# Selective scan on one Trainium2 core: softplus summed in PSUM, one odd group in five multiplied by VectorE, projection begun a third of a step sooner, step sizes in single buffers

## The chip, the cores and the metric

The kernel runs on one core of a Trainium2 chip. A core has TensorE (PE in the profile), VectorE (DVE), ScalarE (ACT), GpSimd (POOL) and SyncE (SP), which here issues all DMAs. The metric is the device time of one execution in microseconds, lower is better; the median of several runs stands for a kernel.

## What is computed

The input x has shape 16 x 64 x 64 x 96, in float32. Two residual layers follow each other. Layer 0 is a group norm, upsampling by Fourier interpolation, two dense layers around a quadratic, a low-pass filter and downsampling. Layer 1, around which the change lies, is a group norm, an input projection, a depthwise 3 x 3 convolution with SiLU, and a selective scan over the 4096 positions in four directions:

```
delta = softplus(dts + dt_bias)                    # per channel and position
h = exp(dt[..., None] * As[None]) * h + (dt * ut)[..., None] * bt[:, :, None, :]
y = einsum('bkdn,bkn->bkd', h, ct)                 # 16 states per channel
```

Four directions x 192 channels x 16 states are 12,288 recurrences of 4096 steps for each of 16 images. A layer norm, a gate and an output projection end the layer.

## The kernel before, in words

The order of instructions on every engine is written out by hand; each engine works its own queue in that order, and semaphores link the queues. There are three generators of background work and one main loop.

**The main loop (scan).** `steps` lists 8 steps per image: four chunks of T = 1024 positions forwards (pair 0), then four backwards (pair 1), 128 steps in all. A step has six blocks (lines 601 to 603), a block has NQ = 4 units j, and so there are 3072 units n, 24 in a step and 192 in an image. A unit holds two groups e = 1 (odd) and e = 0, each 128 recurrences (32 channels x 4 states) over 1024 positions. For a group:

- ScalarE makes the decay exp(delta * a) from SBUF into a PSUM tile `da` (`decay`, L725). There are two such tiles.
- GpSimd multiplies dt * u with B for both groups of a unit at once, from SBUF into SBUF (`drive`, L731: tile `b`, three buffers).
- VectorE runs the recurrence (`recur`, L740 forwards, L742 backwards). For e = 1 the state overwrites `b` in SBUF, for e = 0 it overwrites `da` in PSUM.
- The state is multiplied by C: e = 1 on GpSimd in place (L877)[...], e = 0 on VectorE from PSUM into `b` (L887).
- ScalarE copies the state's last column for the next chunk (`keep`, L748), except in the last chunk of a direction. L877 waits for that copy, since it overwrites what the copy reads.
- TensorE adds up the four states of each channel by 8 matmuls with a 0/1 matrix per group (`read_out`, L764), and `store` (L775) moves the sums out after four units.

The order within one iteration n (lines 869 to 894): scan e = 1 of n, keep, decay (n+1, 1), read_out (n-1), background slot 0, L877 of n, drive (n+2); then scan e = 0 of n, background slot 1, L887 of n, keep, decay (n+1, 0), background slot 2. A buffer of `b` is free for drive (n+2) once read_out (n-1) is done.

**Background work.** In each of the three slots of a unit the class `Background` runs one slice of a generator (up to a `yield`), spread evenly: `step_gen`, and then `ahead_gen` or, once that is finished, `behind_gen`. Slices say how many yields are spread over how many places. `front(mi+1)` is layer 0 and the convolution of the next image; `finish(mi-1)` is layer norm, gate and output projection of the image before; both share SLICES = 540 in 576 places. `project` makes the operands of the next step: it is begun at block 0 and spread as PSLICES = 60 over 59 places, drained at block 5, j = 0.

**project (lines 622 to 677)** works in 2 halves of 512 positions. Three tiles u are fetched, three matmuls (L640) give B, C and the ranks of dt in PSUM, ScalarE copies them to SBUF (L643), and then, for each of three channel tiles, one matmul (L650) gives s, the argument of softplus, in PSUM. Softplus is max(s, 0) + ln(1 + e) - ((1 + e) - 1 - e) with e = exp(-|s|); the last term corrects the rounding of 1 + e. ScalarE computes |s| and e (L658, L659), ln (L661) and 1 + e (L666), VectorE L664, L668 and L669, then dtu = s * u (L672). ScalarE copies delta to SBUF (L674). Both go to HBM (L676, L677). Such a piece occurs 768 times.

**Fetches.** `fetch` (L684) brings dtu and delta of a block, each spread over the four states of a channel, into tiles for both groups: dtu at j = 0 and delta at j = 1 of the block before, from pools of two. `fetch_bc` (L693) brings B and C rows. In `front`, the intermediate of the filter is fetched into two tiles of 44 and 20 columns (lines 408 to 416) and read by L433.

Of the kernel before, what the change touches and what calls it, by code (L numbers as in the profile page):

```python
# [51 lines left out]
C = 96  # L52
HW = 64
# [18 lines left out]
SLICES = 540  # L72
WAIT = -1
HEAVY = 2
PSLICES = 60
# [3 lines left out]
def tile_two_blocks(  # L79
# [103 lines left out]
    b12 = ctx.enter_context(tc.tile_pool(name="b12", bufs=1))  # L183
# [56 lines left out]
    def front(mi):  # L240
# [72 lines left out]
        for p0 in range(0, UPS, PP):  # L313
# [94 lines left out]
        JS = 44  # L408
        s = [
            b18.tile([UPS, JS, C], F32, name="s0", tag="b18"), b12.tile([UPS, HW - JS, C], F32, name="s1", tag="b12")  # L410
        ]
        for _ in range(2):
            yield
        for i, n, first in [(0, JS // 4, k * JS // 4) for k in range(4)] + [(1, 10, 0), (1, 10, 10)]:
            nc.sync.dma_start(out=s[i][:, first:first + n, :], in_=s_d[:, JS * i + first:JS * i + first + n, :])
            yield
# [4 lines left out]
        for j0 in range(0, HW + 8, 8):  # L421
            if done is not None:
                nc.scalar.activation(
                    x1v[:, :, j0 - 8:j0], done.rearrange("c w h -> c h w"), AF.Identity, bias=shift
                )
            if j0 < HW:
                done = bank([C, 8, HW], "e_ps")
                nc.tensor.matmul(
                    done.rearrange("c w h -> c h w"), lhsT=lin, rhs=x1v[:, :, j0:j0 + 8], start=True, stop=False,
                    skip_group_check=True,  # L430
                )
                for j in range(8):
                    nc.tensor.matmul(  # L433
                        done[:, j, :], lhsT=s[(j0 + j) // JS][:, (j0 + j) % JS, :], rhs=down_s, start=False, stop=True,
                        skip_group_check=True,
                    )
            yield
        yield from parts(made["x1"], x1)
# [167 lines left out]
    def scan():  # L606


        with ExitStack() as es:
            pj = es.enter_context(tc.tile_pool(name="sc_pj", bufs=1))  # L610
            up_ = es.enter_context(tc.tile_pool(name="sc_u", bufs=3))
            cp = es.enter_context(tc.tile_pool(name="sc_bc", bufs=5))
            p3 = es.enter_context(tc.tile_pool(name="sc_3", bufs=3))
            p2 = es.enter_context(tc.tile_pool(name="sc_2", bufs=2))
            yp = es.enter_context(tc.tile_pool(name="sc_y", bufs=1))
            stp = es.enter_context(tc.tile_pool(name="sc_st", bufs=2))
            banks.append(es.enter_context(tc.tile_pool(name="b_ps", bufs=2, space=PSUM)))
# [4 lines left out]
            def project(mi, pair, lc, out):  # L622

                out["rows"] = rows = dram.tile([2, 2 * NS, T], F32, name="rows")
                out["delta"] = [dram.tile([128, T], F32, name=f"delta_d{v}") for v in range(3)]
                out["dtu"] = [dram.tile([128, T], F32, name=f"dtu_d{v}") for v in range(3)]
                xs_d = image[mi]["xs"]
                for t in range(0, T, TB):  # L630
                    u = []
                    for v in range(3):
                        uv = up_.tile([128, TB], F32, name="u")
                        nc.sync.dma_start(out=uv, in_=xs_d[v, :, lc * T + t:lc * T + t + TB])
                        u.append(uv)
                    for _ in range(3):
                        yield
                    pp = gps.tile([128, TB], F32, name="pp", tag="g")
                    for v in range(3):
                        nc.tensor.matmul(pp, lhsT=xpt_s[:, pair, v, :], rhs=u[v], start=(v == 0), stop=(v == 2))  # L640
                    yield
                    pr = pj.tile([128, TB], F32, name="pr")
                    nc.scalar.activation(pr, pp, AF.Identity, bias=bumps_s)  # L643


                    for i, v in enumerate((0, 2, 1)):
                        if i == 0:
                            yield
                        s = gps.tile([128, TB], F32, name="s", tag="g")
                        nc.tensor.matmul(s, lhsT=dtw_s[:, pair, v, :], rhs=pr, start=True, stop=True)  # L650
                        if i == 0:
                            for r in range(2):
                                nc.sync.dma_start(
                                    out=rows[r, :, t:t + TB], in_=pr[64 * r:64 * r + 2 * NS, :]
                                )
                        yield
                        e, d = (pj.tile([128, TB], F32, name=k) for k in ("e", "d"))
                        nc.scalar.activation(e, s, AF.Abs)  # L658
                        nc.scalar.activation(e, e, AF.Exp, scale=-1.0)  # L659
                        yield  # L660
                        nc.scalar.activation(d, e, AF.Ln, bias=one_s)  # L661
                        for _ in range(2):
                            yield
                        nc.vector.scalar_tensor_tensor(d, s, 0.0, d, ALU.max, ALU.add)  # L664
                        yield
                        nc.scalar.activation(s, e, AF.Identity, bias=one_s)  # L666
                        yield
                        nc.vector.scalar_tensor_tensor(s, s, -1.0, e, ALU.add, ALU.subtract)  # L668
                        nc.vector.tensor_sub(s, d, s)  # L669
                        dtu = pj.tile([128, TB], F32, name="dtu")  # L670
                        delta = pj.tile([128, TB], F32, name="delta")
                        nc.vector.tensor_mul(dtu, s, u[v])  # L672
                        yield
                        nc.scalar.copy(delta, s)  # L674
                        yield
                        nc.sync.dma_start(out=out["dtu"][v][:, t:t + TB], in_=dtu)  # L676
                        nc.sync.dma_start(out=out["delta"][v][:, t:t + TB], in_=delta)  # L677

            def fetch(what, ctx, bi):

                v, s0, r = blocks[bi]
                t = p2.tile([128, 2, T], F32, name=what)
                for e in (1, 0):
                    nc.sync.dma_start(  # L684
                        out=t[:, e, :],
                        in_=ctx[what][v][32 * (s0 + e):32 * (s0 + e) + 32, :].unsqueeze(1).to_broadcast([32, NQ, T]),
                    )
                return t
# [23 lines left out]
            ops = {(w, 0): fetch(w, ctxs[0], 0) for w in ("dtu", "delta")}  # L712
# [9 lines left out]
            def decay(n, e):  # L722
                k, g = group(n, e)
                da = aps.tile([128, T], F32, name="da")
                nc.scalar.activation(da, ops["delta", n // NQ][:, e, :], AF.Exp, scale=a_s[:, k, g, units[n][2]:units[n][2] + 1])  # L725
                das[n, e] = da

            def drive(n):
                b = p3.tile([128, 2, T], F32, name="b")
                bt = bc[0, blocks[units[n][1]][2], units[n][2]]  # L730
                nc.gpsimd.tensor_mul(b, ops["dtu", n // NQ], bt.unsqueeze(1).to_broadcast([128, 2, T]))  # L731
                bs[n] = b
# [11 lines left out]
            def keep(n, e, h):  # L744
                st, bi, j = units[n]
                if st % NT < NT - 1:
                    end = h[:, T - 1:T] if steps[st][1] == 0 else h[:, 0:1]
                    nc.scalar.copy(states[bi][1][:, e, j:j + 1], end)  # L748
# [77 lines left out]
            last = len(units) - 1  # L826
            for n in range(2):
# [5 lines left out]
            for n, (st, bi, j) in enumerate(units):  # L833
# [11 lines left out]
                if j == 0:  # L845
                    if bi == 0 and st + 1 < len(steps):
                        if steps[st + 1][0] > mi:
                            ahead_gen.drain()
                        step_gen = Background(project(*steps[st + 1], ctxs[st + 1]), PSLICES, 59)
# [3 lines left out]
                if j == 0:  # L853
# [3 lines left out]
                    elif n + NQ <= last:  # L857
                        step_gen.drain()
                        ahead = ctxs[st + 1], 0
                    if ahead:  # L860
                        ops["dtu", m + 1] = fetch("dtu", *ahead)
                elif j == 1:
                    if ahead:
                        ops["delta", m + 1] = fetch("delta", *ahead)
                    if n + NQ <= last and steps[units[n + NQ - 1][0]][1] == 1:
                        st2, bi2, _ = units[n + NQ - 1]
                        y0s[steps[st2][2], bi2] = fetch_y0(steps[st2][2], bi2)

                h = bs[n][:, 1, :]
                recur(n, 1, h)  # L870
                keep(n, 1, h)
                if n < last:
                    decay(n + 1, 1)
                if n:
                    read_out(n - 1)
                slot(0)
                nc.gpsimd.tensor_mul(h, h, bc[1, r, j])  # L877
# [5 lines left out]
                if n and units[n - 1][2] == NQ - 1:  # L883
                    storing = store(n - 1)
# [3 lines left out]
                keep(n, 0, h)  # L888
# [3 lines left out]
                if storing is not None:  # L892
                    next(storing, 0)
                    storing = None

# [9 lines left out]
            read_out(last)  # L905
# [112 lines left out]
```

## Time and profile before

| | us |
|---|---|
| median of 3 runs (21913.64 to 21924.9) | 21916.79 |
| the profiled execution's own time | 21910.69 |
| its span, first to last instruction | 21908.9 |
| PE busy | 15342.2 (70%) |
| ACT busy | 13130.2 (60%) |
| L740, L742: 6144 scans, each | 2.28 to 2.34 |
| L725 decay, each (6144) | 1.116 |
| DMA, mean rate over the span | 195 GB/s |

A row of the page's groups gives line, engine, operation, tiles (output <- inputs), shapes and count; after the bar the busy time in us and the mean of one in ns; after the second bar the time that the engine sat idle just before such instructions, with what ended it. A row of the order of time gives start and length in us, engine, line, operation; in brackets the idle time before it and what ended it. A row of the waits gives who waited for whom: us in total, times, longest. Engines also have weight loads (PEld) and DMA issues (SPq) of their own.

### The profile page before, as it was taken

How to read it: one execution, taken by the hardware profiler on the slowest of the kernel's cores; microseconds unless marked ns; L12 is line 12 of the kernel's file. 1: busy time of each engine (PE TensorE's matmuls, PEld its weight loads, DVE VectorE, ACT ScalarE, POOL GpSimd, SP SyncE). 2: the span in 40 equal slices, each digit the busy share in tenths (PEclk: the TensorE clock that was granted, in tenths of full speed). 3: DMA queues.
4: the chain of work that ended last, by engine and by line, in shares of the span. 5: the costliest groups of instructions: out<-in, count | busy, mean ns of one | idle time of the engine just before them, and what ended most of it. 6: DMA issues, size and time to landing. Idle time of an engine off the chain costs nothing.

```text
span 21908.9 us, 260666 instructions
## 1 busy us (share of the span) xinstructions
PE 15342.2 (70%) x92844; PEld 6324.7 (29%) x92844; DVE 19849.9 (91%) x12829; ACT 13130.2 (60%) x20854; POOL 20900.4 (95%) x6152
## 2 busy tenths in 40 slices
PE   6766767766777677777767677767777677677745
PEld 4322323232232322324233232322323223242211
DVE  0999999999999999999999999999999999999996
ACT  4665656666565665656656566665656656566543
POOL 0999999999999999999999999999999999999997
PEclk7776777877778777777877778777787877778856
DMA  2555565656656566565655656556565655656654
GB/s 80 190 191 188 193 214 194 209 195 200 205 191 215 189 206 201 192 215 192 207 198 194 214 192 209 196 201 206 193 211 189 210 199 198 206 195 208 210 177 134
DMA packets 1851895, 4276.30 MB, mean 195 GB/s; under 512 B 449118, under 2 KB 548350, under 8 KB 1848542
## 3 DMA queue, kind: packets, MB, share of 16 engines
q1 hardware_dynamic: 1850590, 4259.62, 58.1%
q8 instruction: 731, 11.98, 0.2%
q14 instruction: 574, 4.70, 0.1%
HBM read 3380.58 MB, written 878.18 MB: 194 GB/s over the span
## 4 chain that ended last, share of the span: by engine, by line
DVE 36%; POOL 19%; issue 18%; PE 9%; ACT 9%; DMA 7%; SPq 1%; POOLq 0%; DVEq 0%; ACTq 0%
POOL b L731 10%; POOL b L877 10%; DVE da L742 7%; DVE da L740 7%; DVE b L740 6%; DVE b L742 6%; DVE b L887 4%; ACT da L725 4%; DMA u<-xs_d 2%; DVE s L669 2%; DVE dtu L672 2%; DVE s L668 2%; PE y L764 1%; DMA ct<-rows 1%; PE pp L640 1%
## 5 line engine op out<-in xcount | busy, mean ns | idle before, releaser
L731 POOL TENSOR_TENSOR b<-dtu,bt 128x2048 f32<-128x2048 f32 x3072 | 13984.9, 4552 | 584.6 <-DMA dtu<-dtu_d 522.9
L725 ACT ACTIVATE da<-delta,a_s 128x1024 f32<-128x1024 f32 x6144 | 6853.5, 1116 | 2826.6 <-DVE b L887 1185.9
L877 POOL TENSOR_TENSOR b<-b,ct 128x1024 f32<-128x1024 f32 x3072 | 7309.1, 2379 | 259.8 <-ACT new L748 249.5
L764 PE MATMUL y<-b,fold_s 128*32 128x256 f32 x49152 | 4638.9, 492 | 4107.3 <-DVE b L887 3102.6
L887 DVE TENSOR_TENSOR b<-da,ct 128x1024 f32<-128x1024 f32 x3072 | 3752.6, 1222 | 84.5
L764 PEld LDWEIGHTS y<-b,fold_s 128*32 128x32 f32 x49152 | 1353.3, 126 | 7627.7 <-DVE b L887 4083.3
L740 DVE TENSOR_TENSOR_SCAN da<-da,new,b 128x1024 f32<-128x1024 f32 x1152 | 2694.3, 2339 | 252.3 <-ACT da L725 252.3
L740 DVE TENSOR_TENSOR_SCAN b<-da,new,b 128x1024 f32<-128x1024 f32 x1152 | 2698.0, 2342 | 174.1 <-POOL b L731 166.9
L742 DVE TENSOR_TENSOR_SCAN da<-da,new,b 128x1024 f32<-128x1024 f32 x1152 | 2693.8, 2338 | 172.9 <-ACT da L725 172.7
L742 DVE TENSOR_TENSOR_SCAN b<-da,new,b 128x1024 f32<-128x1024 f32 x1152 | 2697.1, 2341 | 151.6 <-POOL b L731 109.5
L748 ACT COPY new<-da 128x1 f32<-128x1 f32 x2304 | 362.3, 157 | 3028.5 <-DVE b L887 3023.2
L473 PE MATMUL c_ps<-xgp,wtap_s 96*128 96x512 f32 (+1 forms) x4608 | 1817.8, 675 | 168.9 <-ACT row L491 164.1
L650 PE MATMUL s<-pr,dtw_s 128*128 128x512 f32 x1536 | 1120.4, 819 | 557.8 <-ACT delta L674 516.7
L377 PE MATMUL o_ps<-w2c_s,hsq 128*100 128x96 f32 x9600 | 1205.3, 293 | 191.9 <-ACT hsq L348 180.1
L365 PE MATMUL h_ps<-xu,w1t_s 96*128 96x500 f32 x1920 | 1147.6, 700 | 244.2 <-ACT hsq L348 108.6
L748 ACT COPY new<-b 128x1 f32<-128x1 f32 x2304 | 432.6, 188 | 1445.7 <-DVE b L742 740.4
L377 PEld LDWEIGHTS o_ps<-w2c_s,hsq 128*100 128x100 f32 x9600 | 1119.5, 203 | 407.4 <-ACT hsq L348 227.7
L640 PE MATMUL pp<-u,xpt_s 128*128 128x512 f32 x1536 | 903.7, 734 | 224.2 <-DMA u<-xs_d 216.0
L742 DVE TENSOR_TENSOR_SCAN b<-da,b 128x1024 f32<-128x1024 f32 x384 | 876.7, 2283 | 133.2 <-ACT da L725 74.8
L473 PEld LDWEIGHTS c_ps<-xgp,wtap_s 96*128 96x128 f32 (+1 forms) x4608 | 631.9, 182 | 1193.3 <-issue 938.6
L740 DVE TENSOR_TENSOR_SCAN da<-da,b 128x1024 f32<-128x1024 f32 x384 | 875.8, 2281 | 106.9 <-ACT da L725 106.9
L742 DVE TENSOR_TENSOR_SCAN da<-da,b 128x1024 f32<-128x1024 f32 x384 | 876.0, 2281 | 105.0 <-ACT da L725 105.0
(120 smaller groups left out, 18077.1 us busy)
## 6 DMA issues: line engine op xcount, KB each, us to landing
dtu<-dtu_d SPq DMA_DIRECT2D x1536, 512.0 KB
delta<-delta_d SPq DMA_DIRECT2D x1536, 512.0 KB
bt<-rows SPq DMA_DIRECT2D x1024, 512.0 KB
ct<-rows SPq DMA_DIRECT2D x1024, 512.0 KB
u<-xs_d SPq DMA_DIRECT2D x896, 256.0 KB
dtu_d<-dtu SPq DMA_DIRECT2D x768, 256.0 KB
delta_d<-delta SPq DMA_DIRECT2D x768, 256.0 KB
xr<-in_x SPq DMA_DIRECT2D x768, 128.0 KB
```

Source lines behind the costliest of these rows:

```text
L365: nc.tensor.matmul(h_ps[j], lhsT=w1t_s[:, 128 * j:128 * (j + 1)], rhs=xu.rearrange("c p q -> c (p q)"), start=True, stop=True,)
L377: nc.tensor.matmul(o_ps[:, p, :], lhsT=hsq[j][:, UPS * p:UPS * (p + 1)], rhs=w2c_s[:, j, :], start=(j == 0), stop=(j == HB - 1),)
L473: nc.tensor.matmul(c_ps[p:p + n], lhsT=wtap_s[:, tap, 128 * i:128 * i + n], rhs=xgp[:, h0:h0 + 8, dx:dx + HW], start=(tap == 0), stop=(tap ...
L640: nc.tensor.matmul(pp, lhsT=xpt_s[:, pair, v, :], rhs=u[v], start=(v == 0), stop=(v == 2))
L650: nc.tensor.matmul(s, lhsT=dtw_s[:, pair, v, :], rhs=pr, start=True, stop=True)
L725: nc.scalar.activation(da, ops["delta", n // NQ][:, e, :], AF.Exp, scale=a_s[:, k, g, units[n][2]:units[n][2] + 1])
L731: nc.gpsimd.tensor_mul(b, ops["dtu", n // NQ], bt.unsqueeze(1).to_broadcast([128, 2, T]))
L740: nc.vector.tensor_tensor_scan(out, da, b, before, ALU.mult, ALU.add)
L742: nc.vector.tensor_tensor_scan(out[:, ::-1], da[:, ::-1], b[:, ::-1], before, ALU.mult, ALU.add)
L764: nc.tensor.matmul(y[32 * q:32 * q + 32, e, :], lhsT=fold_s, rhs=b[:, e, QT * q:QT * q + QT], start=(pair == 0 and j == 0 and e == 0), sto ...
L877: nc.gpsimd.tensor_mul(h, h, bc[1, r, j])
L887: nc.vector.tensor_mul(bs[n][:, 0, :], h, bc[1, r, j])
```

## The change

In words, part by part:

- **SHARE = 5.** In units with n % 5 = 4 the scan of e = 1 writes its state into `da` (PSUM), and VectorE multiplies it by C into `b`. L877 is left out there.
- **Softplus.** ScalarE makes m = max(s, 0), w = 1 - (1 + e) in two instructions, e and d = ln(1 + e); four matmuls with the identity add w + e + d + m in PSUM (the same PSUM buffer as s, after it is read). The three VectorE instructions L664, L668 and L669 and ScalarE's L666 go.
- **keep.** For e = 1 VectorE copies the last column, where the state is in SBUF; ScalarE copies it in the units with n % 5 = 4.
- **project.** Begun at block 5, j = 0 for the step after the next, as 71 slices in 72 places, drained there a step later; u tiles are asked for ahead (four buffers), and their channel order is that of their use. Its HBM tiles come from a pool of three.
- **Buffers.** delta's two groups become single tiles from a pool of three, fetched at j = 1 (e = 1) and j = 3 (e = 0). `b` has four buffers, and read_out and store come a unit later (n-2). y0 is fetched at the end of the unit before its block.
- **front.** The filter's intermediate is fetched in two parts, 40 and 24 columns, into one buffer one after the other; with more yields. SLICES becomes 550.

The diff, cut:

```diff
-SLICES = 540
+SLICES = 550
-PSLICES = 60
+PSLICES = 71
+SHARE = 5
...
+        def fetch_s(first, n):
+            t = b18.tile([UPS, n, C], F32, name="s", tag="b18")
+            for k in range(0, n, 8):
+                nc.sync.dma_start(out=t[:, k:k + 8, :], in_=s_d[:, first + k:first + k + 8, :])
+                yield t, first
+        JS = 40
...
+            if j0 == JS:
+                for s, s_first in fetch_s(JS, HW - JS):
+                    yield
...
+                ahead_u = [fetch_u(v, 0) for v in order]
+                for _ in range(4):
+                    yield
                 for t in range(0, T, TB):
-                    for _ in range(3):
-                        yield
+                    u, ahead_u = dict(zip(order, ahead_u)), []
...
-                        e, d = (pj.tile([128, TB], F32, name=k) for k in ("e", "d"))
+                        e, d, m, w = (pj.tile([128, TB], F32, name=k) for k in ("e", "d", "m", "w"))
                         nc.scalar.activation(e, s, AF.Abs)
                         nc.scalar.activation(e, e, AF.Exp, scale=-1.0)
                         yield
+                        nc.scalar.activation(m, s, AF.Relu)
+                        nc.scalar.activation(w, e, AF.Identity, bias=one_s)
+                        yield
                         nc.scalar.activation(d, e, AF.Ln, bias=one_s)
-                        for _ in range(2):
+                        nc.scalar.activation(w, w, AF.Identity, scale=-1.0, bias=one_s)
+                        yield
+                        s = gps.tile([128, TB], F32, name="s", tag="g")
+                        yield
+                        for k, of in enumerate((w, e, d, m)):
+                            nc.tensor.matmul(s, lhsT=ident_s, rhs=of, start=(k == 0), stop=(k == 3))
+                        for _ in range(3):
                             yield
-                        nc.vector.scalar_tensor_tensor(d, s, 0.0, d, ALU.max, ALU.add)
-                        yield
-                        nc.scalar.activation(s, e, AF.Identity, bias=one_s)
-                        yield
-                        nc.vector.scalar_tensor_tensor(s, s, -1.0, e, ALU.add, ALU.subtract)
-                        nc.vector.tensor_sub(s, d, s)
                         nc.vector.tensor_mul(dtu, s, u[v])
...
-                b = p3.tile([128, 2, T], F32, name="b")
+                b = p4.tile([128, 2, T], F32, name="b")
...
-                    if bi == 0 and st + 1 < len(steps):
-                        if steps[st + 1][0] > mi:
-                            ahead_gen.drain()
-                        step_gen = Background(project(*steps[st + 1], ctxs[st + 1]), PSLICES, 59)
...
                         step_gen.drain()
                         ahead = ctxs[st + 1], 0
+                        next_step(st + 2, mi)
...
                 elif j == 1:
                     if ahead:
-                        ops["delta", m + 1] = fetch("delta", *ahead)
+                        deltas[m + 1, 1] = fetch_delta(*ahead, 1)
+                elif j == 3:
+                    if ahead:
+                        deltas[m + 1, 0] = fetch_delta(*ahead, 0)
...
-                h = bs[n][:, 1, :]
+                odd_here = n % SHARE == SHARE - 1
+                h = das[n, 1] if odd_here else bs[n][:, 1, :]
                 recur(n, 1, h)
-                keep(n, 1, h)
+                if odd_here:
+                    nc.vector.tensor_mul(bs[n][:, 1, :], h, bc[1, r, j])
+                keep(n, 1, h, nc.scalar.copy if odd_here else nc.vector.tensor_copy)
                 if n < last:
                     decay(n + 1, 1)
-                if n:
-                    read_out(n - 1)
+                if n >= 2:
+                    read_out(n - 2)
                 slot(0)
-                nc.gpsimd.tensor_mul(h, h, bc[1, r, j])
+                if not odd_here:
+                    nc.gpsimd.tensor_mul(h, h, bc[1, r, j])
```

`next_step(st, mi)` sets step_gen to `Background(project(...), PSLICES, 3 * per_step)`, 72 places, after draining ahead_gen if the step is one of the next image.

## The prediction

> **What bounds the kernel now.** I read four views in this order: the page's busy times, the groups of instructions, the order of time in the middle of the run, and the list of waits. All durations are of the profiled execution, 21,910.7 us (span 21,908.9), 6 us under the median of the runs, 21,916.8.
>
> The page puts GpSimd (POOL) first and VectorE (DVE) close behind:
>
> ```profile
> PE 15342.2 (70%) x92844; PEld 6324.7 (29%) x92844; DVE 19849.9 (91%) x12829; ACT 13130.2 (60%) x20854; POOL 20900.4 (95%) x6152
> DVE  0999999999999999999999999999999999999996
> POOL 0999999999999999999999999999999999999997
> ```
>
> The missing 5% of POOL is the serial start and end. Busy time by stretch separates them:
>
> ```profile
> 0.00:560.00 560.00, 384.38 (x2340) 229.72 (x2340) 60.93 (x84) 237.48 (x395) 45.58 (x21) 0.78 0.26 81
> 560.00:21760.00 21200.00, 14818.93 (x90216) 6054.10 (x90216) 19772.50 (x12722) 12868.05 (x20420) 20854.84 (x6132) 0.76 0.59 199
> ```
>
> The columns after the length are PE, PEld, DVE, ACT, POOL, clock. In the 21,200 us of the scan POOL idles 345 us and DVE 1,427 us. So POOL sets the pace, with DVE 5% behind it. A unit (n in the main loop; 3072 of them) has one multiplication L877 and one L731 on POOL, and on DVE two scans (b for e=1, then da for e=0) and L887:
>
> ```profile
> L731 POOL TENSOR_TENSOR b<-dtu,bt 128x2048 f32<-128x2048 f32 x3072 | 13984.9, 4552 | 584.6 <-DMA dtu<-dtu_d 522.9
> L877 POOL TENSOR_TENSOR b<-b,ct 128x1024 f32<-128x1024 f32 x3072 | 7309.1, 2379 | 259.8 <-ACT new L748 249.5
> L887 DVE TENSOR_TENSOR b<-da,ct 128x1024 f32<-128x1024 f32 x3072 | 3752.6, 1222 | 84.5
> ```
>
> ```profile
> 10009.03 0.69 DVE L668 SCALAR_TENSOR_TENSOR s<-s,e 128x512 f32<-128x512 f32 x1
> 10009.12 2.35 POOL L877 TENSOR_TENSOR b<-b,ct 128x1024 f32<-128x1024 f32 x1
> ...
> 10009.76 0.70 DVE L669 TENSOR_TENSOR s<-d,s 128x512 f32<-128x512 f32 x1
> 10010.49 0.69 DVE L672 TENSOR_TENSOR dtu<-s,u 128x512 f32<-128x512 f32 x1
> 10011.10 2.34 DVE L740 TENSOR_TENSOR_SCAN b<-da,new,b 128x1024 f32<-128x1024 f32 x1
> ...
> 10011.44 4.50 POOL L731 TENSOR_TENSOR b<-dtu,bt 128x2048 f32<-128x2048 f32 x1
> ```
>
> POOL goes from L877 to L731 in 2.32 us and the next L877 starts at 10015.91: 6.79 us a unit, with no gap. The waits show what DVE loses when it isn't waiting for POOL:
>
> ```profile
> DVE da L740 <- ACT da L725: 359.2, 285, 5.9
> DVE da L742 <- ACT da L725: 277.6, 267, 2.4
> POOL b L877 <- ACT new L748: 249.5, 168, 4.0
> DVE b L740 <- POOL b L731: 216.8, 270, 1.1
> DVE b L742 <- POOL b L731: 166.5, 198, 1.1
> ```
>
> **What the Trainium skill says.** (1) "SBUF — State Buffer", Who interferes with whom: GpSimd's SBUF ports are VectorE's second pair; a VectorE instruction with two SBUF inputs, or one in a two-port mode, and a GpSimd instruction lock each other out for a whole instruction. The trace agrees: L259, with two SBUF inputs, takes 245 ns before POOL starts and 1278 ns otherwise. It starts at 570.27 and ends at 571.55, just after POOL's L731 (566.91 to 571.44). (2) "VectorE: DVE Perf Modes", What auto-detection actually checks: a one-source instruction from SBUF to SBUF takes the two-port mode if its outermost non-unit sizes are even or equal. Whether one element per partition counts isn't said, and no row of before shows such a copy. (3) "TensorE: Matmul & The Clock Gate", What's actually happening: TensorE has a half and a full clock, by activity. The trace agrees: weight loads of consecutive L640 passes are 0.43 us apart at 9992 us, passes of L473 0.86 us apart at 12,008 us. (4) Price: "ScalarE: Activation LUTs", What ACT_TABLE_LOAD costs: 280 + 0.833 x 512 = 706 ns with a bias operand; L661 shows 711.
>
> **The change, part by part.**
>
> *One odd group in five.* n % 5 = 4 holds in 614 units. POOL loses 614 x 2.32 = 1,424 us. DVE gains 614 x 1.22 = 750 us (row L887: same sizes, one input in PSUM, so no lock).
>
> *Softplus in PSUM.* 768 pieces (16 images x 8 steps x 2 x 3). DVE loses L664, L668 and L669; from start to start 0.60 + 0.73 + 0.73 = 2.06 us, x 768 = 1,582 us. L672 stays. ACT trades L666 for three: Relu (0.58, as L658, a read of PSUM) and two Identity (0.71 each), net +1.33 us x 768 = 1,020 us. PE gains four matmuls, eight passes a piece at 0.43 to 0.86 us: 3.4 to 6.9 us, 2,640 to 5,300 us in all. ACT and PE have room on average (60% and 70% now); what this costs is in bursts, below.
>
> *States of odd groups copied by DVE* except in those 614 units. The last of four steps keeps none, so 0.75 x 2,458 = 1,843 copies of 128x1. The trace has no such copy. Low end: the 0.12 us of L258, a one-element instruction with PSUM input, 221 us in all. High end: each waits for POOL's instruction in progress (the lock), worked out under the rivals. I take the low end. POOL's 249.5 us of waits for ACT's copy go. Neither end is under zero, since an instruction is added.
>
> *Projection a third of a step sooner.* It starts at block 5 instead of the next block 0 and has 72 places for 70 slices instead of 60 for 58, ending at the same block 5. DVE and POOL have no instruction added by it. On the DMA queue (SP) u is asked for up to a piece earlier, which covers L640's 216 us of waits for it; the stores come two places after their producer, so SP waits less at their head. I cost these at nothing; they hide behind the scan as now, whose DMA share is 0.59.
>
> *Single buffers.* delta's halves are fetched at j=1 and j=3. The second uses the half that the decay for unit 4m+3 frees and is needed after L887 of that unit: from that decay's end about one unit plus a scan and a multiplication less 1.2 us, 8.7 us. Two halves of 512 KB at the page's 195 GB/s are 5.4 us, an estimate. It fits with 3 us to spare; if each were 1 us late, 768 blocks cost DVE up to 768 us. Queued behind such a fetch on SP are bt, ct and the stores.
>
> *The rest.* read_out goes to n-2 with a fourth b, so drive(n+2) still waits for the read-out of the same iteration, but that one's data are a unit older. This takes away PE's waits for L887 (3,102.6 us), nothing on the path. s in two fetches of one buffer makes front 12 slices longer (389 of 550 in 576 places: ready at place 407, needed at 492), cover enough; only the serial first front pays about 10 us. The first projection, serial too, has some 20 us more of PE passes: +30 us in all. y0 is asked for some two units later, still two units (13 us) ahead of its reader, which moves back by one.
>
> **The sum.** POOL in the scan: 20,855 - 1,424 = 19,431 busy, plus at most its 345 idle: 19,776. DVE busy: 19,772 - 1,582 + 750 + 221 = 19,161. To it come pauses before dependent instructions (0.03 us after a scan, where other pairs have none; 3072 + 2457 times): about 190. Then waits for ACT's decays, 637 today: much of it comes where ACT's queue holds its own copy and the projection's pr, both eased; I keep half, 320. Bursts: ACT's next instruction after the eight passes can be 4.5 us (0.56 a pass at the mean clock 0.77) less a slot (2.1 us) and about 1 us of PE's lead late: 1.4; a decay has 2.25 (scan) - 0.16 - 1.12 = 0.97 to spare. That leaves 0.4 to 0.5 us of stall; I take 0.5 x 768 = 384. DVE: 19,161 + 190 + 320 + 384 = 20,055. It now ends last, 280 us behind POOL, so waits for each other come in both directions; the odd group swings their distance by some 2.8 us in five units, against 3.6 us that the b buffers allow. I add 0.5%, 100. Outside the scan: 560 + 149 + 30 = 739. **20,055 + 100 + 739 = 20,894: I say 20,900**, 4.6% faster.
>
> **The rivals.**
>
> *The copies lock* (chance 0.25). Each of the 1,843 copies waits until POOL's L731 ends, then L877 waits for the copy: 4.52 + 2.32 + 0.2 = 7.0 us per plain unit. Of five units three are such, 21.0; the pair around an odd group goes at DVE's pace, 2 x 5.76 + 1.26 + 0.12 = 12.9. That is 6.78 a unit, 6.42 in steps without copies, 6.69 on average, against 21,200 / 3072 = 6.90 now: 0.21 x 3072 = 645 less, some 65 back for ACT: 21,330. For it: L259. Against it: two-port mode for one element is not shown.
>
> *POOL alone ends it* (0.13). No DVE stall beyond today's slack: 19,776 + 739 = 20,515. For it: prefetch of u and a later read-out. Against it: DVE's sums are as high.
>
> *PE's bursts hold ACT, and so DVE: slower* (0.06). The path is eight passes, then front's matmul behind them, ACT waiting on that in order, the decay behind it, the scan. At 0.86 us a pass the burst is 6.9, the stall 6.9 - 2.1 - 1 - 0.97 = 2.8 us. It decides from (21,911 - 20,894) / 768 + 0.5 = 1.8 us a piece on; at 2.8 us the time is 20,894 + 2.3 x 768 = 22,660. Against it: a busier PE gets the full clock (0.97 in the serial end).
>
> **Numbers.** Forecast 0.53, lock 0.25, POOL alone 0.13, slower 0.06, and 0.03 for a lock or late halves that eat the whole gain, within 0.2% (about what a measurement of this kernel can tell from no change). Faster 0.91. The range runs from a little under the POOL-alone case, 20,400, to above the lock case with some late fetches, 21,500.
>
> **What would show it.** POOL's L877 with 2,458 instructions and its waits for ACT near zero; a DVE copy of 0.1 us (if its mean is over 0.5 us, the lock is there); DVE busy over 95% in the scan; PE near 88%; DVE's waits for L725 near 700 us. The forecast is wrong if the new copy is long, if DVE's waits for L725 pass 1,500 us, or if delta's halves show as a releaser.

## The result, and the profile after

| | before | after |
|---|---|---|
| median, us | 21,915.2 (21,909.5 to 21,924.9) | 21,649.6 (21,642.2 to 21,674.6) |
| profiled execution, span, us | 21,908.9 | 21,650.1 |

The ratio is 0.988, with a 95% interval from 0.9863 to 0.9897. The change is faster by 1.2%. The forecast was 4.6% (20,900 us), so three quarters of the expected gain didn't come.

The page's busy times and slices of the kernel after; below them the stretch of the scan (columns as before: length, PE, PEld, DVE, ACT, POOL, clock, DMA share, GB/s):

```profile
PE 16910.3 (78%) x98988; PEld 7341.1 (34%) x98988; DVE 19532.7 (90%) x12983; ACT 13726.8 (63%) x20546; POOL 19514.3 (90%) x5538
DVE  0999999999999999999999999999999999999997
POOL 0999999999999999999999999999999999999996
```

```profile
560.00:21500.00 20940.00, 16362.41 (x96392) 7057.80 (x96390) 19488.18 (x12905) 13480.87 (x20153) 19492.11 (x5525) 0.86 0.60 202
```

POOL lost 1,386 us of work, as intended, and DVE 317. The two are now equally busy, and **both idle**: 1,448 us for POOL (345 before) and 1,452 for DVE (1,427). A digit of 9 in the slices hides that. Before, POOL was hardly ever short of work. Now neither is the bound alone.

The groups that carry the change:

```profile
L761 POOL TENSOR_TENSOR b<-dtu,bt 128x2048 f32<-128x2048 f32 x3072 | 13898.6, 4531 | 1341.2 <-PE y L794 617.3
L917 POOL TENSOR_TENSOR b<-b,ct 128x1024 f32<-128x1024 f32 x2458 | 5798.8, 2359 | 631.1 <-DVE new L778 291.2
L909 DVE TENSOR_TENSOR b<-da,ct 128x1024 f32<-128x1024 f32 x614 | 751.9, 1225 | 49.4 <-DVE da L770 1.4 <-DVE da L772 0.5
L778 DVE COPY new<-b 128x1 f32<-128x1 f32 x1844 | 283.6, 154 | 63.1
L236 DVE TENSOR_TENSOR nb<-nmean,rg 96x1 f32<-96x1 f32 x32 | 160.8, 5025 | 331.0 <-ACT rg L233 330.8
```

The first four are the prediction's steps, with two differences: a copy takes 154 ns and not 120, and POOL's waits for the copies stay (291 us for VectorE's, where it waited 250 us for ScalarE's). The fifth is an instruction that the change doesn't touch: 32 products of 96 numbers, at 5,025 ns each, where they took 855 before:

```profile
L236 DVE TENSOR_TENSOR nb<-nmean,rg 96x1 f32<-96x1 f32 x32 | 27.3, 855 | 293.3 <-ACT rg L233 293.3
```

The waits of the kernel after (total us, times, longest):

```profile
POOL b L761 <- PE y L794: 617.3, 365, 8.3
DVE da L770 <- ACT da L755: 478.3, 421, 3.4
ACT t L310 <- PE o_ps L377: 427.2, 187, 7.3
ACT da L755 <- DMA delta<-delta_d: 369.1, 141, 19.2
DVE dtu L691 <- PE s L686: 352.9, 130, 135.5
DVE da L772 <- ACT da L755: 332.4, 292, 4.0
POOL b L917 <- DVE new L778: 291.2, 224, 12.2
ACT hsq L348 <- PE h_ps L365: 288.4, 192, 5.2
```

Four of these have grown or are new. ScalarE waits for TensorE (L310: 118 us before, L348: 65) and for delta (19 us before, once). POOL waits for the read-out (16 us before). VectorE waits longest for decays again, though its waits for POOL have gone from 383 us to under 60.

### The profile page after: what moved, and what is told of

It reads as the page before. It is cut to its first block, busy times and chain, and to the rows that moved or that the text cites. A ratio compares the mean times of both kernels' runs of the same rounds, so it can differ in the third digit from the quotient of the medians.

```text
span 21650.1 us, 273738 instructions
## 1 busy us (share of the span) xinstructions
PE 16910.3 (78%) x98988; PEld 7341.1 (34%) x98988; DVE 19532.7 (90%) x12983; ACT 13726.8 (63%) x20546; POOL 19514.3 (90%) x5538
## 5 line engine op out<-in xcount | busy, mean ns | idle before, releaser
L761 POOL TENSOR_TENSOR b<-dtu,bt 128x2048 f32<-128x2048 f32 x3072 | 13898.6, 4531 | 1341.2 <-PE y L794 617.3
L917 POOL TENSOR_TENSOR b<-b,ct 128x1024 f32<-128x1024 f32 x2458 | 5798.8, 2359 | 631.1 <-DVE new L778 291.2
L794 PE MATMUL y<-b,fold_s 128*32 128x256 f32 x49152 | 3623.5, 420 | 331.3 <-DVE b L927 141.1
L770 DVE TENSOR_TENSOR_SCAN da<-da,new,b 128x1024 f32<-128x1024 f32 x1383 | 3247.0, 2348 | 386.8 <-ACT da L755 361.7
L772 DVE TENSOR_TENSOR_SCAN da<-da,new,b 128x1024 f32<-128x1024 f32 x1382 | 3242.8, 2346 | 230.3 <-ACT da L755 212.4
L686 PE MATMUL s<-w,ident_s 128*128 128x512 f32 x1536 | 1212.9, 882 | 1345.3 <-ACT w L681 1265.6
L772 DVE TENSOR_TENSOR_SCAN b<-da,new,b 128x1024 f32<-128x1024 f32 x922 | 2157.9, 2340 | 45.9 <-ACT da L755 36.3
L770 DVE TENSOR_TENSOR_SCAN b<-da,new,b 128x1024 f32<-128x1024 f32 x921 | 2156.3, 2341 | 13.3 <-ACT da L755 8.5
L482 PE MATMUL c_ps<-xgp,wtap_s 96*128 96x512 f32 (+1 forms) x4608 | 1694.3, 635 | 163.2 <-ACT row L500 158.7
L666 PE MATMUL s<-pr,dtw_s 128*128 128x512 f32 x1536 | 1005.9, 741 | 1000.2 <-ACT pr L659 495.9
L377 PE MATMUL o_ps<-w2c_s,hsq 128*100 128x96 f32 x9600 | 1061.3, 270 | 187.0 <-ACT hsq L348 161.8
L772 DVE TENSOR_TENSOR_SCAN da<-da,b 128x1024 f32<-128x1024 f32 x461 | 1055.9, 2291 | 120.4 <-ACT da L755 120.0
L770 DVE TENSOR_TENSOR_SCAN da<-da,b 128x1024 f32<-128x1024 f32 x460 | 1053.7, 2291 | 121.0 <-ACT da L755 116.5
L377 PEld LDWEIGHTS o_ps<-w2c_s,hsq 128*100 128x100 f32 x9600 | 992.2, 182 | 393.0 <-ACT hsq L348 218.9
L686 PE MATMUL s<-e,ident_s 128*128 128x512 f32 x1536 | 1088.3, 800 | 0.0
```

What stands on the lines that cost most here:

```text
L377: nc.tensor.matmul(o_ps[:, p, :], lhsT=hsq[j][:, UPS * p:UPS * (p + 1)], rhs=w2c_s[:, j, :], start=(j == 0), stop=(j == HB - 1),)
L482: nc.tensor.matmul(c_ps[p:p + n], lhsT=wtap_s[:, tap, 128 * i:128 * i + n], rhs=xgp[:, h0:h0 + 8, dx:dx + HW], start=(tap == 0), stop=(tap ...
L686: nc.tensor.matmul(s, lhsT=ident_s, rhs=of, start=(k == 0), stop=(k == 3))
L761: nc.gpsimd.tensor_mul(b, dtus[n // NQ], bt.unsqueeze(1).to_broadcast([128, 2, T]))
L770: nc.vector.tensor_tensor_scan(out, da, b, before, ALU.mult, ALU.add)
L772: nc.vector.tensor_tensor_scan(out[:, ::-1], da[:, ::-1], b[:, ::-1], before, ALU.mult, ALU.add)
```

## Where VectorE idles

I classed every idle stretch of VectorE in the scan of the profiled execution by what ended just before the next instruction started (within 0.1 us; the 12 us after the last scan are left out):

| kernel after, VectorE idle in the scan | us |
|---|---|
| scans whose decay began only as VectorE's instruction before ended | 457 |
| other late decays | 518 |
| dtu (L691), for the four matmuls | 165 |
| gaps of under 0.06 us between instructions | 165 |
| POOL's b | 60 |
| L909, L236 and the rest | 75 |

Classed the same way, the kernel before has 527 us in the first row. That row looks odd, so here it is in the order of time:

```profile
10014.96 2.34 DVE L770 TENSOR_TENSOR_SCAN b<-da,new,b 128x1024 f32<-128x1024 f32 x1
...
10017.33 1.12 ACT L755 ACTIVATE da<-delta,a_s 128x1024 f32<-128x1024 f32 x1 [2.10 <-DVE b L770]
10017.33 0.15 DVE L778 COPY new<-b 128x1 f32<-128x1 f32 x1
...
10018.48 2.36 DVE L770 TENSOR_TENSOR_SCAN da<-da,new,b 128x1024 f32<-128x1024 f32 x1 [1.00 <-ACT da L755]
```

ScalarE sat idle for 2.10 us. It waited for the scan of e = 1, which has nothing to do with the decay of e = 0, except that both tiles `da` are the same PSUM buffer. There are two buffers in one pool, and they aren't handed out strictly in turn: now and then a decay gets the buffer of the decay just before it and not the one before that. The addresses in the built program show that in 556 of 6,144 decays after, and in 530 before. Each can cost about a whole decay, here 1.0 us. The kernel before has it too:

```profile
9995.60 2.35 DVE L740 TENSOR_TENSOR_SCAN b<-da,new,b 128x1024 f32<-128x1024 f32 x1 [0.93 <-POOL b L731]
...
9997.99 1.12 ACT L725 ACTIVATE da<-delta,a_s 128x1024 f32<-128x1024 f32 x1 [2.65 <-DVE b L740]
...
9999.14 2.36 DVE L740 TENSOR_TENSOR_SCAN da<-da,new,b 128x1024 f32<-128x1024 f32 x1 [1.19 <-ACT da L725]
```

L236 is the second find. First VectorE, then POOL in the same stretch of the kernel after:

```profile
10377.02 12.17 DVE L236 TENSOR_TENSOR nb<-nmean,rg 96x1 f32<-96x1 f32 x1
10389.11 2.34 DVE L770 TENSOR_TENSOR_SCAN da<-da,new,b 128x1024 f32<-128x1024 f32 x1
```

```profile
10373.43 4.51 POOL L761 TENSOR_TENSOR b<-dtu,bt 128x2048 f32<-128x2048 f32 x1
10377.92 2.35 POOL L917 TENSOR_TENSOR b<-b,ct 128x1024 f32<-128x1024 f32 x1
10380.23 8.94 POOL L761 TENSOR_TENSOR b<-dtu,bt 128x2048 f32<-128x2048 f32 x2
```

L236 reads two tiles in SBUF. It starts in POOL's first instruction and ends at 10,389.19, with the end of POOL's fourth (10,389.17). The Trainium skill, "SBUF — State Buffer", Who interferes with whom, calls this an exclusive lock of the shared port pair. The trace agrees and adds that a waiting VectorE instruction can lose several turns while POOL's queue runs without a pause. This is one of the two longest of the 32. All 30 that fall beside POOL's work end within 0.03 us of the end of a POOL instruction, before and after. The median is 4.56 us after, 0.50 before.

## The experiments

My theory after the comparison: POOL's work is no longer the bound, VectorE's is, and stalls of VectorE that lay in its slack before now count in full. Three stalls were suspected: the shared PSUM buffers, the lock of L236 and the bursts of eight TensorE passes. The expectations call this theory 1. There were two rivals: TensorE, with its added matmuls, sets the end (theory 2), or POOL (GpSimd) still ends it, and its waits for PE and for the copies are the cost (theory 3).

**One suspect at a time, on the kernel after.** First, a PSUM buffer of its own for each of the two groups.

```diff
-aps = ...tile_pool(name="sc_aps", bufs=2, space=PSUM)
+aps = ...tile_pool(name="sc_aps", bufs=1, space=PSUM)
-da = aps.tile([128, T], F32, name="da")
+da = aps.tile([128, T], F32, name="da", tag=f"da{e}")
```

> The changed kernel with one PSUM buffer for the decays of e=1 and one for e=0, instead of two that are handed out to whichever decay comes next. In the changed kernel 556 of 6144 decays are given the buffer of the decay just before them, and so wait for the scan that still reads it. Theory 1 (VectorE now sets the end and loses about 460 us to such decays): 300 to 450 us less, about 21,270 us. Theory 2 (TensorE with its added matmuls sets the end): less than 100 us. Theory 3 (GpSimd still sets the end): less than 100 us.

Measured: 21,295.7 us (ratio to before 0.9714, 0.9699 to 0.9728), **354 less** than after. Its waits for decays:

```profile
DVE da L772 <- ACT da L755: 244.1, 178, 5.3
DVE da L770 <- ACT da L755: 227.1, 205, 3.3
```

811 us in 713 waits became 471 in 383. Of the other waits in the list above none changes by more than 160 us, so most of the gain is this stall's. The first row of the table above falls from 457 to 51 us. Theory 1 holds here.

Second, L236 on ScalarE.

```diff
-nc.vector.tensor_mul(nb, nmean, rg)
+nc.scalar.activation(nb, nmean, AF.Identity, scale=rg)
```

> The changed kernel with the product nb of the group norm (L236) on ScalarE. It is the VectorE instruction with two SBUF inputs that took 5.0 us on average, 161 us in all, in the changed kernel against 0.86 us before, because it waits for GpSimd. Theory 1: VectorE gets 150 us back, 100 to 190 us less, about 21,500 us. Theories 2 and 3: within 40 us of the changed kernel.

Measured: 21,532.3 us (0.9824, 0.9808 to 0.984), **117 less**. It takes 279 ns there, and VectorE's busy time falls by 135 us, to 19,397.6. POOL's work (19,518.3 us) and its waits for the read-out (616 us) stay as they were, so this time is VectorE's own, as theory 1 has it.

Third, one of the four matmuls: delta is max(s, 0) alone, the three other terms of softplus aren't added.

```diff
-for k, of in enumerate((w, e, d, m)):
-    nc.tensor.matmul(s, lhsT=ident_s, rhs=of, start=(k == 0), stop=(k == 3))
+nc.tensor.matmul(s, lhsT=ident_s, rhs=m, start=True, stop=True)
```

> The changed kernel with one of the four matmuls that add softplus up, so that delta is max(s, 0) alone; everything else stays. TensorE loses 2304 matmuls of two passes, some 2,000 us of work. Theory 2: 500 to 1,000 us less. Theory 1: only VectorE's waits for the sum (165 us) and a part of the late decays go, 100 to 350 us less. Theory 3: GpSimd's 617 us of waits for the read-outs go, 300 to 600 us less.

Measured: 21,201.0 us (0.9669, 0.9655 to 0.9684), **449 less**. Waits of L348 for TensorE go from 288 to 92 us, and of L310 from 427 to 281. This is a miss for theory 1, which had 100 to 350 us, and for theory 2, which had 500 to 1,000. It lies in the range of theory 3: POOL's waits for the read-out fall too, from 617 to 226 us. The granted clock falls from 0.857 to 0.803, so what is left of TensorE's work isn't the same either.

Fourth, no odd groups on VectorE (`SHARE = 10000`), which leaves the rest of the change.

> The changed kernel without the odd groups on VectorE: all 3072 are multiplied by GpSimd. GpSimd gets 614 x 2.32 = 1,424 us back, VectorE loses 752 us and gets 461 copies. Theory 1: GpSimd is then the bound with 20,835 us of work and few waits, about 21,700 us, so that the odd groups alone are worth next to nothing in the changed kernel. Theory 2: TensorE is as before, 21,600 us. Theory 3: 22,300 us or more.

Measured: 22,004.7 us, 1.0036 of before (1.0023 to 1.0049): slower than after by 355, and than before by 0.4%. It lies between theory 1 (about 21,700) and theory 3 (22,300 or more), so neither had the size. POOL is busy 20,907.0 us (95%), and VectorE waits for it:

```profile
DVE b L770 <- POOL b L761: 392.8, 524, 1.0
DVE b L772 <- POOL b L761: 368.6, 527, 1.0
```

So softplus in PSUM and the other parts gain nothing while POOL is the bound.

**Together, and the same edits on the kernel before.** The two edits that keep the whole computation (buffers and L236):

> The changed kernel with both: a PSUM buffer for the decays of each e, and nb on ScalarE. Theory 1 (VectorE's own time sets the end): the two add up, 355 + 117 us less than the changed kernel, about 21,180 us. Theory 3 (GpSimd is met as the bound on the way): less than the sum, 21,250 us or more.

Measured: 21,177.0 us (0.966, 0.9646 to 0.9675), 473 less than after. Alone they gave 354 and 117, the sum of which is 471: they add up. With the single matmul as well:

> The same, with one of the four matmuls that add softplus up (delta is max(s, 0) alone). Theory 1: the third saving of 450 us adds to the two, 20,730 us, near the forecast of 20,900 us. If GpSimd or the unavoidable part of VectorE's work is met on the way: 20,850 us or more.

Measured: 20,773.3 us (0.9473, 0.9457 to 0.9489), 876 less than after and below the forecast. The third saving is 404 us here, not 450, so the time lies between the two expectations, nearer to the first. VectorE's idle time in the scan (560 to 20,630 us) is 740 us.

The odd groups of n % 5 = 4 alone, in the kernel before (state into `da`, multiplied by VectorE, and everything else unchanged):

> The kernel before with one part of the change alone: in units with n % 5 = 4 VectorE multiplies the odd group from PSUM, GpSimd leaves it out; ScalarE keeps copying the states, softplus stays on VectorE. Theory 1: VectorE becomes the bound with 20,520 us of work and about 800 us of waits for decays, 21,800 to 22,300 us, no gain. Theory 3 (GpSimd sets the end): 20,500 us, all of its 1,424 us gained.

Measured: 22,206.4 us (1.013, 1.0115 to 1.0145), **slower** by 283, as theory 1 had it (theory 3 had 20,500). VectorE has 20,574.1 us of work there. POOL, with 19,512.7, waits:

```profile
POOL b L881 <- ACT new L748: 1370.3, 737, 6.4
```

The separate PSUM buffers alone, in the kernel before:

> The kernel before with a PSUM buffer for the decays of each e; 530 of its decays are given the buffer of the decay just before. Its GpSimd sets the end and idles only 345 us in the scan, so all theories expect little: 0 to 150 us less than the kernel before, against 355 us less in the changed kernel.

Measured: 21,824.7 us (0.9957, 0.9942 to 0.9971): 98 less, where the same edit takes 354 from the kernel after. VectorE's waits for decays in `da` fall from 637 to 229 us, and its waits for POOL rise from 383 to 651. Most of the cured stall came back as waits for POOL.

**What is in the bursts, the copies and the fetches.** The last four kernels start from the version with both edits (21,177 us). First, the four matmuls in pairs: the same TensorE work, never eight passes in a row. The second pair stands where all four stood, the first two slots earlier.

```diff
-yield
 s = gps.tile([128, TB], F32, name="s", tag="g")
-yield
-for k, of in enumerate((w, e, d, m)):
-    nc.tensor.matmul(s, lhsT=ident_s, rhs=of, start=(k == 0), stop=(k == 3))
+for k, of in enumerate((m, e)):
+    nc.tensor.matmul(s, lhsT=ident_s, rhs=of, start=(k == 0), stop=False)
+for _ in range(2):
+    yield
+for k, of in enumerate((d, w)):
+    nc.tensor.matmul(s, lhsT=ident_s, rhs=of, start=False, stop=(k == 1))
```

> The kernel after with separate PSUM tiles for the decays of the two groups and nb on ScalarE (a run before: 21,177 us), and the four matmuls of softplus in two pairs: m and e as soon as they are ready, d and w two slots later. TensorE does the same work, but never eight passes in a row. If the burst is what holds ScalarE's queue and with it the decays, most of what leaving out three of the four matmuls gave (449 us after, 404 with banks and nb) comes without leaving anything out: 20,800 to 21,000 us. If the amount of TensorE work matters (the sum comes later, every queue behind TensorE is longer), it stays at 21,150 to 21,200 us.

Measured: 20,885.0 us (0.9531, 0.9515 to 0.9547), **292 less**. ScalarE's waits for TensorE, which were 422 (L310) and 269 us (L348):

```profile
ACT t L310 <- PE o_ps L377: 277.1, 129, 4.8
ACT hsq L348 <- PE h_ps L365: 137.4, 137, 3.2
```

So nearly three quarters of what leaving out three matmuls gives (404 us in this version) comes with the same work in two pieces. It comes by more than one path: VectorE's waits for decays fall from 648 to 500 us, those for the sum (dtu) from 400 to 273, and POOL's for the read-out from 453 to 273. How the 292 us divide among these isn't shown.

Second, all columns of odd groups copied by ScalarE again.

```diff
-keep(n, 1, h, nc.scalar.copy if odd_here else nc.vector.tensor_copy)
+keep(n, 1, h, nc.scalar.copy)
```

> As the same version (21,177 us), but the last columns of the odd groups are all copied by ScalarE, as in the kernel before. VectorE loses 284 us of copies and about 75 us of pauses before them. If VectorE alone is the bound, 20,800 to 20,900 us. If what the copies took away, POOL's multiplication L917 waiting for ScalarE's queue (249 us before), now counts since POOL and VectorE are equally late, 21,150 to 21,350 us.

Measured: 21,089.0 us (0.9626, 0.9611 to 0.964), 88 less. It lies between the two expectations: VectorE has 295 us less to do (19,094.9), and POOL's L917 waits 480 us for the column, where it waited 179. Here the copies on VectorE cost a little more than they bring.

Third, the second half of delta asked for right after decay (n+1, 1) at j = 2, the decay that frees its buffer, and no longer at the head of unit j = 3.

```diff
     decay(n + 1, 1)
+if j == 2 and ahead:
+    deltas[m + 1, 0] = fetch_delta(*ahead, 0)
...
-elif j == 3:
-    if ahead:
-        deltas[m + 1, 0] = fetch_delta(*ahead, 0)
```

> As the same version (21,177 us), but the second half of delta is asked for in the unit before, right after the decay that frees its buffer is issued, and so ahead of the other transfers that the queue issues in between. ScalarE waits 461 us for delta, 175 times, in the version without this edit. If those waits come from the place of the request in the queue, they fall to under 200 us and the time to 20,950 to 21,080 us. If the transfer itself is too slow for its one buffer, or the waits lie beside other waits, 21,130 to 21,200 us.

Measured: 21,016.3 us (0.9587, 0.9573 to 0.9602), **161 less**. ScalarE's waits for delta, before the edit and with it, and the longest wait of the queue before it:

```profile
ACT da L755 <- DMA delta<-delta_d: 460.6, 175, 19.3
ACT da L755 <- DMA delta<-delta_d: 35.5, 15, 19.4
SPq L695 <- DVE dtu L691: 3729.6, 627, 15.1
```

The transfer was fast enough. It was asked for too late: between the two places in the queue other requests can stand that wait for something else. The store of dtu (L695) held the queue most of all, 3,730 us in 627 waits; how much of that fell just before a fetch of delta isn't shown.

Last, all four edits that keep the computation and were found to help (buffers, L236, pairs, earlier request).

> All four edits that kept the whole computation and helped, on the kernel after: separate PSUM tiles for the decays of the two groups, nb on ScalarE, the four matmuls in two pairs, the second half of delta asked for right after the decay that frees its buffer. If the four stalls are separate ones, each is worth what it was alone (354, 117, 292, 161 of 21,650 us): 20,725 us, between 20,690 and 20,780. If the pairs and the earlier request cure the same late decays, 20,840 to 20,880. Below 20,242 us (POOL's 19,502 us and 740 outside the scan) nothing can come of it.

Measured: **20,727.9 us** (0.9459, 0.9443 to 0.9475), 922 less than after and 5.4% less than before; four stalls that add up. The scan of this version (columns as above):

```profile
560.00:20580.00 20020.00, 16146.28 (x96330) 6825.55 (x96330) 19334.59 (x12863) 13513.96 (x20140) 19458.80 (x5519) 0.87 0.63 211
```

POOL idles 561 us of it, VectorE 685. ScalarE's copies (88 us in another version) weren't tried on top.

## Why the prediction was wrong

The direction was right: POOL's share fell, and stalls and work of VectorE came to count. That VectorE ends last, "280 us behind POOL", was not: the two are equally busy and equally idle. And the size was not right. In the prediction's own terms:

| step | forecast, us | measured, us |
|---|---|---|
| POOL busy in the scan | 19,431 | 19,492 |
| VectorE busy in the scan | 19,161 | 19,488 |
| VectorE idle in the scan (190 + 320 + 384 + 100) | 994 | 1,452 |
| outside the scan | 739 | 710 |
| sum of the last three | 20,894 | 21,650 |

The idle time term by term: pauses 190, measured 165 (the prediction's 0.03 us x 5,529 is 166, not 190); waits for decays 320 + 384, measured 975; waits between VectorE and POOL 100, measured 60; the wait for the sum in PSUM, L909, L236 and the rest have no term, measured 240.

- **The failing step is the waits for decays.** The sum has "I keep half, 320" and 384 for the bursts, "near 700 us" in all. The list of waits of the kernel after has 993 (779 before, of which the prediction counted the 637 in `da`). It kept half because it put them down to ScalarE's queue, "both eased". The runs showed another cause, which the change leaves alone: in the kernel before, 527 us of VectorE's idle time came before scans whose decay could begin only as VectorE's own instruction ended. The lines that the prediction showed don't say why a decay was late; the order of time would have shown ScalarE idle before it. The shared buffer is worth 354 us in the kernel after.
- **"Single buffers" failed too.** They have no term in the sum, since "it fits with 3 us to spare". The estimate, 5.4 us of transfer in 8.7 us, was of the transfer. What the request stands behind in the queue was not looked at, only what stands behind it. Worth 161 us of the 768 that the prediction allowed; "delta's halves show as a releaser" was its own sign of being wrong, and they do.
- **VectorE's busy time** was 327 us short: 63 are the copies, at 154 ns and not 120, and 133 are L236, to which the prediction gave no thought, though it had read the lock off L259. L259 itself fell from 1,215 to 244 ns. Of the remaining 131, 33 are work that lay in the first 560 us before (VectorE is busy 61 us there before and 28 after), and 75 come from instructions back to back, which overlap in the records by 615 us in all before and by 541 after. The last 23 aren't broken down.
- **The bursts** are of about the right size. From its first start to its last end a burst takes 4.73 us on average (768 of them, 3.6 to 6.8), forecast 4.5. Its stalls were put at 384 us. Three of the four matmuls are worth 449 (404 in the version with both edits), and 292 of that comes back when the burst is broken up. The mechanism, ScalarE held and so the decay late, is a part of it: with the burst broken up the waits for decays fall by 148 us and the wait for the sum, which had no term, by 128.
- **TensorE's clock.** TensorE's share is 78% and not 88%, and not for the four matmuls' sake: L686 takes 3,635 us, inside the forecast's 2,640 to 5,300. But all its other work fell from 15,342 to 13,276 us while the mean granted clock rose from 0.766 to 0.857. If all of it went with the clock, 15,342 x 0.766 / 0.857 = 13,713 would be left, an estimate, so the clock accounts for most of the fall. The prediction's page for the two clock speeds, the Trainium skill's "TensorE: Matmul & The Clock Gate", What's actually happening, has the clock follow activity; the trace agrees, and I hadn't applied it to the work that was there before.
- **The copies** aren't locked: 1,844 of them at 152 to 156 ns, 1,408 of them wholly inside a POOL instruction (one at 10,003.86 us, in L761). That rival is refuted, and so is its 21,330, though it was the nearest to the result. "POOL alone" and "slower" didn't occur.

The account closes: 20,894 + 354 (buffers) + 117 (L236) + 161 (delta) = 21,526, and the version with these three cured ran in 21,016, 122 above the forecast. Of those 122, 63 are the copies and up to 65 the bursts (449 less 384). That they are exactly this is argued, not shown; the wait for the sum is in them too.

The deeper error is that the waits of before were read as the cost of a stall. They were taken while POOL paced the kernel, and the same PSUM edit is worth 98 us there and 354 here. A stall that is slack today is a price tomorrow, once the bound goes. The rival theory, that POOL still ends it, doesn't hold by itself: the edit of L236 takes work from VectorE alone, 135 us, and the time falls by 117. But POOL isn't far off either. In the version with ScalarE's copies 295 us less on VectorE gave 88, and the worth of the single matmul fell in theory 3's range. What part of the bursts' worth came over which of the two engines isn't told apart here.

## What to carry to other kernels

When a change takes work from the engine that sets the pace, price the next engine from its own idle time, cause by cause, and ask for each late producer what it was waiting for: if it sat idle until the consumer's previous instruction ended, look for a shared buffer that the names don't show. A fetch costs what it stands behind in the queue, not only its transfer. In this kernel a small instruction with two SBUF inputs on VectorE belonged elsewhere once POOL's queue ran with few pauses, and a long accumulation was better issued in pieces, since other engines wait in order behind TensorE.

## What the runs showed of the hardware

- A VectorE product of 96 x 1 with two SBUF inputs took up to 12.17 us beside POOL, through the rest of one POOL instruction and three whole ones. ScalarE did the same work in 279 ns.
- A one-element copy from SBUF to SBUF on VectorE took 154 ns beside POOL and never waited for it (1,844 times, 152 to 156 ns).
- Relieving one engine of two did harm (1.3% slower with the odd groups alone, 0.4% with all the rest), and both together helped.
